# Cross-attention block on one core: a quarter of the W1 product by seven block products, and another order of the sum behind the W2 product

## The chip, the cores and the metric

The kernel runs on one core of a Trainium2 chip. The metric is device time in microseconds (us) of one execution. Five engines work side by side, each through its own list of instructions in the order written: TensorE (PE in the profile, with PEld for its weight loads), VectorE (DVE), ScalarE (ACT), GpSimd (POOL) and SyncE (SP), which here issues nearly all DMAs. They wait for each other by semaphores.

## What is computed

128 sequences of 128 tokens with 256 features pass one cross-attention block with 16 heads, two layer norms and a two-layer network with 1024 hidden features:

```python
q = (query @ Wq + bq).reshape(b, s, 16, 16).transpose(0, 2, 1, 3)     # k, v likewise, from the context
scores = jnp.einsum('bhqd,bhkd->bhqk', q, k) / 4
scores = jnp.where(j < i, scores, -1e30)                              # strictly below the diagonal
attn = softmax(scores).at[:, :, 0, :].set(0.0)
x = layer_norm(query + (attn @ v) @ Wo + bo, ln1_g, ln1_b)
ffn = jax.nn.relu(x @ W1 + b1) @ W2 + b2
out = layer_norm(x + ffn, ln2_g, ln2_b)
```

The part that the change touches is the line with `ffn`. All is float32.

## The kernel before

Two sequences make a pair, p = 0 to 63. From p = 7 on the function `step(p)` (line 1212) is one turn of a software pipeline: it does the scores and the softmax of pair p, projects the keys and queries of p + 1, weighs the values of p - 2 and sends them through Wo and the first norm, does the hidden layer of p - 3, the W2 product of p - 4 and the last norm of p - 5. The order is written out by hand: the framework keeps each engine's instructions in the order in which the calls stand. Steps 0 to 6 (`third` to `sixth`) fill the pipeline, `behind` (line 1278) empties it.

On PE one step is: `weigh` (L483, L493), `scores_both` (L376), `queries` (L261), `attention_out` (L512), `keys` (L261), `values` (L301), `second_by_seven` (L794), `hidden` (L699).

The W2 product is already done by seven block products: with the 1024 hidden features cut into even and odd blocks of 128, and the 256 tokens and the 256 outputs into halves, a product of 2 x 2 blocks needs seven block products instead of eight (Winograd's form of Strassen's scheme). Its sums of operands are `combine_hidden` (L780 to L783, on POOL) and once `combine_w2`; `second_by_seven` runs the seven products, each over four pairs of feature blocks, 128 columns wide, into two banks, `py` and `pz`. In each product, one empty instruction (`empty`, L215) follows the first call. `sum_of_seven` (line 813) adds the seven results and the residual `x1b` on DVE: four additions at L823 that each take one 128-wide part of `py` into 512, 384 or 256 elements of `t2`, and one at L831 for three parts of `pz`. Each of them has one operand in PSUM.

`hidden` (line 688) does the W1 product: eight feature blocks of 128, each as two calls of 256 columns (one for each half of the 256 inputs), two blocks to a bank; banks 2, 3, 4, 0 in turn; ACT then adds the bias and applies relu into `hT` (L707). A call in float32 shows as two records in the trace.

On DVE a step is: masks and maxima of the scores (L390, L743, L747, L754), sum and statistics of the first norm (L538, L525, L526), the softmax's sums and reciprocals (L421, L422), the block transposes `turn_x1` (L663) and `tokens` (L247), one `turn` (L436), `sum_of_seven`, two more `turn`, the statistics of the second norm (L525, L526). On POOL: deviation of the second norm (L532, L533, L577), `combine_hidden`, `add_bo` (L254), deviation of the first norm (again L532, L533, L577), three multiplies of the softmax by its reciprocal sums (`sums`, L423), `residual1` (L566, L569), `finish` (L597, L598). On ACT: the copy of the weighed values (L505), 32 exponentials (L762), queries (L272), first norm (L554), keys (L291), `values_out` (two copies L311, two L316), second norm (`norm2`, L591), eight relus (L707). On SP: `bring` (16 moves of the transposed softmax, L451), `store` (L606), loads, and the moves of `turn_x1` (L239, L242).

In step 7 alone, `norm2`, `finish` and `store` of pair 1 stand at the head of the step as well. The eight PSUM banks are used by fixed number; the scores of the second half of the queries take banks 0 to 3, those of the first half banks 6, 7, 4, 5, and a step's scores begin with banks 4 and 5. Queries go to bank 4, keys to 0, values to 1, `po` to 5, the weighed values to 7.

Of the kernel before, what the change touches and what calls it, by code (L numbers as in the profile page):

```python
# [19 lines left out]
def tile_cross_attention_block(  # L20
# [22 lines left out]
    nc = tc.nc  # L43
    B, S, D = x.shape
# [4 lines left out]
    KC = D // P  # L49
    FC = DFF // P  # L50
    TP = 2 * P
    NS = P // 32
# [10 lines left out]
    const = ctx.enter_context(tc.tile_pool(name="const", bufs=1))  # L63
    loads = ctx.enter_context(tc.tile_pool(name="loads", bufs=3))
# [60 lines left out]
    load_tokens(0, slice(0, 2))  # L125
    wk = weight(Wk, "wk")
    wq = weight(Wq, "wq")
    c_first = const.tile([P, 4, D], F32, tag="c_first", name="c_first")
# [81 lines left out]
    def at_bank(i, name):  # L210
        return psum.tile([P, 512], F32, tag=f"b{i}", name=name)
# [39 lines left out]
    def add_bo(p):  # L251
        st = states[p]
        st["xb"] = proj.tile([P, 2, D], F32, tag="xb", name=f"xb_{p}")
        nc.gpsimd.tensor_tensor(  # L254
            st["xb"], tokens_of[p // 2][:, p % 2 * 2 : p % 2 * 2 + 2], bov_r[:, None, :].to_broadcast([P, 2, D]), ALU.add
        )
# [47 lines left out]
                )  # L304

    def values_out(p):
        st = states[p]
        pv = st.pop("pv")
        st["vz"], st["vd"] = vzs[p % 2], vds[p % 2]
        for s in range(2):  # L310
            nc.scalar.copy(  # L311
                st["vz"][:, s, :, 0:4:3, :],
                pv[:, s * D : (s + 1) * D].rearrange("p (r e d) -> p r e d", e=2, d=DK),
            )
        for e in range(2):
# [69 lines left out]
    def mask(p, hi, rs):  # L385
        st = states[p]
        n = P if hi else HP
        no = neg.rearrange("p u j -> p (u j)") if hi else neg[:, 1, :]
        for r in rs:
            nc.vector.tensor_tensor(  # L390
                st["sm", hi][:, 4 * r : 4 * r + 4, :],
                st["sps", hi][r][:, : 4 * n].rearrange("p (n j) -> p n j", j=n),
                no[:, None, :].to_broadcast([P, 4, n]),
                ALU.add,
            )
# [389 lines left out]
    def second_by_seven(p):  # L785

        st = states[p]
        hT, hs = st["hT"], st["hS"]
        py = st["py"] = at_bank(6, f"py_{p}")
        pz = st["pz"] = at_bank(7, f"pz_{p}")  # L790

        def product(out, left, right, after):
            for k in range(FC // 2):
                nc.tensor.matmul(  # L794
                    out, left(k), right(k), start=(k == 0), stop=(k == FC // 2 - 1)
                )
# [10 lines left out]
        product(pz[:, 2 * P : 3 * P], raw(1, 1), lambda k: wt[:, 3, k], 1)  # L807
        product(py[:, 3 * P :], lambda k: hs[:, 0, k], lambda k: wt[:, 0, k], 1)
        product(py[:, 2 * P : 3 * P], lambda k: hs[:, 2, k], lambda k: wt[:, 2, k], 1)
        product(py[:, P : 2 * P], lambda k: hs[:, 1, k], lambda k: wt[:, 1, k], 1)  # L810
        product(pz[:, P : 2 * P], lambda k: hs[:, 3, k], weights(1, 1), 1)

    def sum_of_seven(p):

        st = states[p]
        t2 = st["t2"] = ffn.tile([P, 2, D], F32, tag="t2", name=f"t2_{p}")
        t = t2.rearrange("p s (h d) -> p (s h) d", h=2)
        py, pz = st.pop("py"), st.pop("pz")
        x1b = st.pop("x1b").rearrange("p s (h d) -> p (s h) d", h=2)

        def add(to, of, at):
            n = to.shape[1]
            nc.vector.tensor_tensor(  # L823
                to, of, py[:, None, at * P : (at + 1) * P].to_broadcast([P, n, P]), ALU.add
            )
# [5 lines left out]
        nc.vector.tensor_tensor(  # L831
            t[:, :3], t[:, :3], pz[:, : 3 * P].rearrange("p (n d) -> p n d", d=P), ALU.add
        )

    def second_half(p, s):

# [331 lines left out]
    def sixth(p):  # L1168

        weigh(p - 2)  # L1170
        context(p - 2)
        scores_both(p)
        add_bo(p - 1)
        mask(p, 0, B)
# [36 lines left out]

    def step(p):
        last = p == NP - 1
        weigh(p - 2)
        context(p - 2)
        scores_both(p)
        if p == 7:
            norm2(p - 6)
        combine_hidden(p - 4, POOL_ALONE)
        if p == 7:  # L1220
            finish(p - 6)
            store(p - 6)
# [148 lines left out]
```

## Time and profile before

| | us |
|---|---|
| median of three runs | 1527.93 (1526.05 to 1528.2) |
| the profiled execution | 1528.67 |
| its span, first to last instruction | 1527.0 |
| PE busy | 1514.3 |
| DVE busy | 1332.4 |
| POOL busy | 1255.9 |
| ACT busy | 1118.3 |

A line of the timeline has the start, the length from the first start to the last end, the engine, the line of the kernel, the operation, what it writes and reads, the shape and the count; in brackets, the idle time before it and what ended it. A line of the groups has, behind the bar, the busy time of the group in us and the mean ns of one instruction. A line of the chain of waits has start, share of the chain in us and the piece. "Idle" on an engine that is not the bound costs nothing.

### The profile page before, as it was taken

To read this page: it belongs to the slowest core of one execution; us is meant where nothing else is said; L and a number is where in the kernel's file an instruction comes from. 1 tells how busy PE (TensorE), PEld (TensorE's weight loads), DVE (VectorE), ACT (ScalarE), POOL (GpSimd) and SP (SyncE) were. 2 spreads that over 40 slices of the span, in tenths; PEclk is the share of its full clock that TensorE was granted. 3 is DMA by queue.
4 is the path that set the end of the run, shared out by engine and by line. 5 is a ranking of instruction groups with operands and counts; after the bars stand their busy time and mean duration, and the time that the engine had idled before them with its cause. 6 is when DMAs were issued, how large, how long until landed. Compare 5 with 4: busy or idle time off the path is not lost.

```text
span 1527.0 us, 47892 instructions
## 1 busy us (share of the span) xinstructions
PE 1514.3 (99%) x17926; PEld 1360.6 (89%) x17926; DVE 1332.4 (87%) x2498; ACT 1118.3 (73%) x3391; POOL 1255.9 (82%) x1282
## 2 busy tenths in 40 slices
PE   8999999999999999999999999999999999999998
PEld 7788998998989989989989899899899898998997
DVE  7989988988988988889889889889898898898885
ACT  5668777877877877778778778777777787787752
POOL 6876988888888888888888888888888888888883
PEclk9999999999999999999999999999999999999999
DMA  9356665555656656655556666566566566564441
GB/s 192 87 120 141 154 156 132 135 136 132 143 139 138 143 120 141 148 132 135 137 134 142 145 134 136 132 136 148 134 136 138 128 141 147 133 144 109 115 112 49
DMA packets 415285, 204.24 MB, mean 134 GB/s; under 512 B 282448, under 2 KB 383056, under 8 KB 415056
## 3 DMA queue, kind: packets, MB, share of 16 engines
q1 hardware_dynamic: 412768, 199.34, 56.7%
q8 instruction: 144, 2.36, 0.7%
q10 hardware_dynamic: 2288, 1.85, 0.5%
q14 instruction: 85, 0.70, 0.2%
HBM read 70.26 MB, written 33.29 MB: 68 GB/s over the span
## 4 chain that ended last, share of the span: by engine, by line
PE 94%; DVE 3%; POOL 1%; DMA 1%; issue 1%; ACT 0%; SPq 0%; POOLq 0%; DVEq 0%
PE ph L699 28%; PE py L794 14%; PE pz L794 10%; PE pq L261 7%; PE po L512 7%; PE pv L301 7%; PE pk L261 7%; PE pss L376 6%; PE pc L493 4%; PE pc L483 2%; DVE tb L436 1%; PE py L719 0%; DMA x1t<-tbx 0%; DVE sm L390 0%; DVE su L421 0%
## 5 line engine op out<-in xcount | busy, mean ns | idle before, releaser
L699 PE MATMUL ph<-x1T,w 128*128 128x256 f32 x2048 | 453.6, 380 | 0.7 <-DMA x1T<-x1t 0.7
L699 PEld LDWEIGHTS ph<-x1T,w 128*128 128x128 f32 x2048 | 385.0, 190 | 50.9 <-issue 1.2
L423 POOL TENSOR_TENSOR sm<-sm,rs 128x1024 f32<-128x1024 f32 x192 | 359.3, 1898 | 3.9 <-DVE rs L422 3.3
L762 ACT ACTIVATE sm<-pss,nmx 128x128 f32<-128x128 f32 x944 | 249.9, 414 | 127.3 <-DMA pT<-tb 81.0
L707 ACT ACTIVATE hT<-ph,b1e_c 128x256 f32<-128x256 f32 x504 | 209.1, 467 | 171.3 <-PE ph L699 161.3
L762 ACT ACTIVATE sm<-sm,nmx 128x64 f32<-128x64 f32 x944 | 232.2, 337 | 5.1 <-DVE nmx L754 0.3
L421 DVE TENSOR_REDUCE su<-sm 128x8 f32<-128x1024 f32 (+1 forms) x192 | 225.8, 1176 | 4.0 <-ACT sm L409 3.8
L436 DVE STREAM_TRANSPOSE tb<-sm 128x1024 f32<-128x1024 f32 x186 | 221.0, 1214 | 0.0
L390 DVE TENSOR_TENSOR sm<-pss,neg 128x256 f32<-128x256 f32 (+1 forms) x276 | 108.2, 435 | 121.2 <-PE pss L376 115.4
L532 POOL TENSOR_SCALAR ve<-mv 128x2 f32<-128x2 f32 x127 | 28.7, 226 | 191.7 <-DVE mv L526 190.9
L794 PE MATMUL py<-wt,hS 128*128 128x128 f32 x1440 | 170.6, 275 | 0.0
L794 PEld LDWEIGHTS py<-wt,hS 128*128 128x128 f32 x1440 | 165.7, 192 | 0.0
L747 DVE TENSOR_REDUCE nmx<-pss 128x4 f32<-128x512 f32 x236 | 150.8, 680 | 0.0
L261 PE MATMUL pq<-xT,wq 128*128 128x256 f32 x504 | 125.5, 392 | 0.5 <-DVE sm L390 0.5
L291 ACT ACTIVATE kT<-pk,bkh,half 128x256 f32<-128x256 f32 x252 | 120.3, 558 | 4.0 <-PE pk L261 4.0
L512 PE MATMUL po<-wo,cxT 128*128 128x256 f32 x512 | 121.3, 380 | 0.7 <-ACT cxT L505 0.7
L301 PE MATMUL pv<-wv,cT 128*128 128x256 f32 x512 | 121.0, 380 | 0.0
L261 PE MATMUL pk<-cT,wk 128*128 128x256 f32 x504 | 119.2, 380 | 0.0
L512 PEld LDWEIGHTS po<-wo,cxT 128*128 128x128 f32 x512 | 97.1, 190 | 14.3 <-ACT cxT L505 1.2
L261 PEld LDWEIGHTS pq<-xT,wq 128*128 128x128 f32 x504 | 90.9, 190 | 20.8 <-issue 9.6
L301 PEld LDWEIGHTS pv<-wv,cT 128*128 128x128 f32 x512 | 97.4, 190 | 13.0
L261 PEld LDWEIGHTS pk<-cT,wk 128*128 128x128 f32 x504 | 95.9, 190 | 13.0 <-issue 0.2
(135 smaller groups left out, 2966.6 us busy)
## 6 DMA issues: line engine op xcount, KB each, us to landing
pT<-tb SPq DMA_DIRECT2D x976, 96.0 KB
x1t<-tbx SPq DMA_DIRECT2D x252, 64.0 KB
x1T<-x1t SPq DMA_DIRECT2D x63, 256.0 KB
out_dram<-t SPq DMA_DIRECT2D x63, 256.0 KB
xb<-in_x_dram SPq DMA_DIRECT2D x124, 128.0 KB
cb<-in_ctx_dram SPq DMA_DIRECT2D x124, 128.0 KB
x<-in_x_dram SPq DMA_DIRECT2D x31, 512.0 KB
w<-in_L_xattn_W_dram SPq DMA_DIRECT2D x2, 1024.0 KB
```

Of the source, the lines that this page charges most:

```text
L261: nc.tensor.matmul(ps[:, m * TP : (m + 1) * TP], w[:, k, m * P : (m + 1) * P], src[:, k, :], start=(k == 0), stop=(k == KC - 1),)
L291: nc.scalar.activation(st["kT"][:, m, e, :], pk[:, m * TP : (m + 1) * TP], AF.Identity, bias=bkh[:, m, e : e + 1], scale=half[:, e : e + 1],)
L301: nc.tensor.matmul(pv[:, s * D : (s + 1) * D], st["cT"][:, k, s * P : (s + 1) * P], wv[:, k, :], start=(k == 0), stop=(k == KC - 1),)
L421: nc.vector.tensor_reduce(su, sm[:, part, :], AX.X, ALU.add)
L423: nc.gpsimd.tensor_tensor(sm[:, part, :], sm[:, part, :], rs[:, :, None].to_broadcast([P, part.stop - part.start, n]), ALU.mult,)
L436: nc.vector.transpose(st["tb"][:, :, at : at + 256].rearrange("p j (n a) -> p n j a", a=32), st["sm", hi].rearrange("p h j -> p (h j)")[:, ...
L512: nc.tensor.matmul(po[:, s * D : (s + 1) * D], cxT[:, k, s, :], wo[:, k, :], start=(k == 0), stop=(k == KC - 1),)
L699: nc.tensor.matmul(ph[:, i * TP : (i + 1) * TP].rearrange("p (s i a) -> p s i a", s=2, a=32), w1[:, k, (f + i) * P : (f + i + 1) * P], st[ ...
L707: nc.scalar.activation(st["hT"][:, f + i, :], ph[:, i * TP : (i + 1) * TP], AF.Relu, bias=(b1e_c if p else b1_c)[:, f + i : f + i + 1], sc ...
L747: nc.vector.tensor_reduce(st["nmx", 1][:, 4 * r : 4 * r + 4], st["sps", 1][r].rearrange("p (n j) -> p n j", j=P), AX.X, ALU.max, negate=True,)
L762: nc.scalar.activation(sm[:, h, :], src, AF.Exp, bias=nmx[:, h : h + 1], scale=1.0)
L794: nc.tensor.matmul(out, left(k), right(k), start=(k == 0), stop=(k == FC // 2 - 1))
```

## The change

Hidden feature blocks 0 and 1 are no longer computed by eight calls of 256 columns, but by seven block products of 128 columns in the scheme above: the two feature blocks, the two sequences of the pair (`s`) and the two halves of the input are the 2 x 2 blocks. Blocks 2 to 7 stay as they were (`plain`). This needs

- `combine_w1`, once, in the sixth step: four subtractions of weights on POOL;
- `combine_normed` in each step: four additions and subtractions of 128 elements on POOL, behind `add_bo`;
- seven calls of 128 columns on PE (`Hidden.run`);
- on ACT, a copy of the first product into `hT` (`keep`);
- on DVE, five additions (`u2`, `u3`, `rest`) that build the four blocks in `hT`, each with one product in PSUM; the relu of blocks 0 and 1 then reads and writes `hT`.

The sum behind the W2 product is another one: ACT copies the first product into a small tile `u` (`keep_first`), and DVE makes six additions, four of them on 128 or 256 elements; the third and the fourth add `x1b` and `u`, both in SBUF.

`values_out` is cut in two, with ACT's copies of `u` and of the first product between; `norm2` stands behind the additions of the hidden layer; the plain blocks go to banks 4, 0 and 5. The empty instructions of the W2 product are 9, 9, 9, 8, 8, 8, 8 instead of one in each. The first context tile `c_first` uses a buffer of the load pool instead of its own. `behind` keeps the old `hidden` and `sum_of_seven`.

```diff
     def values_out(p):
-        st = states[p]
-        pv = st.pop("pv")
+        spread_values(p)
+        stack_values(p)
...
-        product(py[:, :P], raw(0, 0), weights(0, 0), 1)
-        product(pz[:, :P], raw(1, 0), weights(1, 0), 1)
...
+        product(py[:, :P], raw(0, 0), weights(0, 0), 9)
+        product(pz[:, :P], raw(1, 0), weights(1, 0), 9)
...
+    def combine_normed(p):
+
+        st = states[p]
+        x1T = st["x1T"]
+        xs = st["xS"] = ffn.tile([P, 4, NS, 32], F32, tag="xS", name=f"xS_{p}", bufs=1)
+        nc.gpsimd.tensor_tensor(xs[:, 0], x1T[:, 1, :, 0, :], x1T[:, 1, :, 1, :], ALU.add)
+        nc.gpsimd.tensor_tensor(xs[:, 2], x1T[:, 0, :, 0, :], x1T[:, 1, :, 0, :], ALU.subtract)
+        nc.gpsimd.tensor_tensor(xs[:, 1], xs[:, 0], x1T[:, 0, :, 0, :], ALU.subtract)
+        nc.gpsimd.tensor_tensor(xs[:, 3], x1T[:, 0, :, 1, :], xs[:, 1], ALU.subtract)
...
+        def run(self, which):
...
+            ps = self.of(which)
+            for i in range(NI):
+                nc.tensor.matmul(
+                    ps[:, i * P : (i + 1) * P].rearrange("p (n a) -> p n a", a=32),
+                    left(i), right, start=True, stop=True,
+                )
...
+        def keep(self):
+            nc.scalar.copy(self.h[:, 0, 0], self.one(1))
+
+        def u2(self):
+            nc.vector.tensor_tensor(self.h[:, 1, 0], self.h[:, 0, 0], self.one(6), ALU.add)
+
+        def u3(self):
+            nc.vector.tensor_tensor(self.h[:, 1, 1], self.h[:, 1, 0], self.one(7), ALU.add)
+            nc.vector.tensor_tensor(self.h[:, 0, 1], self.h[:, 1, 1], self.one(4), ALU.add)
+
+        def rest(self):
+            odd = self.hT[:, 1 : 2 * NI : 2].rearrange("p i (s t) -> p i s t", s=2)
+            nc.vector.tensor_tensor(
+                odd, odd, self.one(5)[:, :, None, :].to_broadcast([P, NI, 2, P]), ALU.add
+            )
+            low = self.h[:, :, 0]
+            nc.vector.tensor_tensor(
+                low, low, self.of(2, 2).rearrange("p (e i t) -> p e i t", e=2, i=NI), ALU.add
+            )
...
+    def keep_first(p):
+        u = states[p]["u"] = ffn.tile([P, 3, P], F32, tag="u", name=f"u_{p}", bufs=1)
+        nc.scalar.copy(u[:, 0], states[p]["py"][:, :P])
+
+    def sum_of_products(p):
...
+        add(u[:, 1], u[:, 0], py[:, P : 2 * P])
+        add(u[:, 2], u[:, 1], py[:, 2 * P : 3 * P])
+        add(t[:, :3], x1b[:, :3], u)
+        add(t[:, 3], x1b[:, 3], u[:, 2])
+        add(t[:, 1::2], t[:, 1::2], py[:, None, 3 * P :].to_broadcast([P, 2, P]))
+        add(t[:, :3], t[:, :3], pz[:, : 3 * P].rearrange("p (n d) -> p n d", d=P))
...
         add_bo(p - 1)
+        combine_normed(p - 3)
         load_ahead(p)
...
         values(p)
-        values_out(p)
-        norm2(p - 5)
         sums(p, 1, ONE)
         sums(p, 1, TWO)
         sums(p, 0, ALL)
         turn_x1(p - 2)
         residual1(p - 3)
         second_by_seven(p - 4)
-        hidden(p - 3, range(FC))
+        spread_values(p)
+        keep_first(p - 4)
+        h = Hidden(p - 3)
+        h.run(1)
+        h.run(6)
+        h.run(7)
+        h.run(4)
+        h.keep()
+        stack_values(p)
...
         turn(p, 1, 0)
-        sum_of_seven(p - 4)
+        sum_of_products(p - 4)
+        h.u2()
+        h.u3()
+        h.run(2)
+        h.run(3)
+        h.run(5)
+        h.rest()
+        norm2(p - 5)
+        h.plain([2, 3], 4)
+        h.relu(2)
+        h.relu(3)
+        h.plain([4, 5], 0)
+        h.relu(4)
+        h.relu(5)
         turn(p, 1, 1)
+        for f in range(2 * NI):
+            h.relu(f)
+        h.plain([6, 7], 5)
+        h.relu(6)
+        h.relu(7)
         turn(p, 0, 0)
```

More of the change, by code (lines that the diff above doesn't have):

```diff
@@ L127, in tile_cross_attention_block @@
     wq = weight(Wq, "wq")
-    c_first = const.tile([P, 4, D], F32, tag="c_first", name="c_first")
+    c_first = loads.tile([P, 4, D], F32, tag="cb2", name="c_first", bufs=2)
     nc.scalar.dma_start(c_first[:, 0:2], c[0:2].rearrange("b p d -> p b d"))
@@ L306, in values_out, with spread_values @@
     def values_out(p):
+        spread_values(p)
+        stack_values(p)
+    def spread_values(p):
         st = states[p]
-        pv = st.pop("pv")
+        pv = st["pv"]
         st["vz"], st["vd"] = vzs[p % 2], vds[p % 2]
@@ L314, in values_out, with stack_values @@
             )
+    def stack_values(p):
+        st = states[p]
+        pv = st.pop("pv")
         for e in range(2):
@@ L803, in weights @@
             return lambda k: w2[:, 2 * k + e, h * P : (h + 1) * P]
-        product(py[:, :P], raw(0, 0), weights(0, 0), 1)
-        product(pz[:, :P], raw(1, 0), weights(1, 0), 1)
[L807 to L811, printed above, removed]
+        product(py[:, :P], raw(0, 0), weights(0, 0), 9)
+        product(pz[:, :P], raw(1, 0), weights(1, 0), 9)
+        product(pz[:, 2 * P : 3 * P], raw(1, 1), lambda k: wt[:, 3, k], 9)
+        product(py[:, 3 * P :], lambda k: hs[:, 0, k], lambda k: wt[:, 0, k], 8)
+        product(py[:, 2 * P : 3 * P], lambda k: hs[:, 2, k], lambda k: wt[:, 2, k], 8)
+        product(py[:, P : 2 * P], lambda k: hs[:, 1, k], lambda k: wt[:, 1, k], 8)
+        product(pz[:, P : 2 * P], lambda k: hs[:, 3, k], weights(1, 1), 8)
     def sum_of_seven(p):
@@ L833, in sum_of_seven, with combine_w1 @@
         )
+    NI = 1
+    w1t = const.tile([P, 4, NI, P], F32, tag="w1t", name="w1t")
+    def combine_w1():
+        w = w1.rearrange("p k (i e f) -> p k e i f", e=2, f=P)[:, :, :, :NI]
+        nc.gpsimd.tensor_tensor(w1t[:, 0], w[:, 0, 1], w[:, 0, 0], ALU.subtract)
+        nc.gpsimd.tensor_tensor(w1t[:, 1], w[:, 1, 1], w1t[:, 0], ALU.subtract)
+        nc.gpsimd.tensor_tensor(w1t[:, 2], w[:, 1, 1], w[:, 0, 1], ALU.subtract)
+        nc.gpsimd.tensor_tensor(w1t[:, 3], w[:, 1, 0], w1t[:, 1], ALU.subtract)
@@ new lines, in tile_cross_attention_block, with __init__, of, one @@
+    class Hidden:
+        WHERE = {1: (2, 0), 6: (2, 1), 7: (2, 2), 4: (2, 3), 2: (3, 0), 3: (3, 1), 5: (3, 2)}
+        def __init__(self, p):
+            st = states[p]
+            self.p, self.x1T, self.xs = p, st["x1T"], st["xS"]
+            self.hT = st["hT"] = ffn.tile([P, FC, TP], F32, tag="hT", name=f"hT_{p}", bufs=1)
+            self.h = self.hT[:, : 2 * NI].rearrange("p (i e) (s t) -> p e s i t", e=2, s=2)
+            self.banks, self.plains = {}, {}
+        def of(self, which, n=1):
+            at, n0 = self.WHERE[which]
+            if at not in self.banks:
+                self.banks[at] = at_bank(at, f"phs_{self.p}_{at}")
+            return self.banks[at][:, n0 * NI * P : (n0 + n) * NI * P]
+        def run(self, which):
+            raw = lambda s, k: self.x1T[:, s, :, k, :]
+            given = lambda k, e: lambda i: w1[:, k, (2 * i + e) * P : (2 * i + e + 1) * P]
+            xs, ws = lambda i: self.xs[:, i], lambda n: (lambda i: w1t[:, n, i])
+            right, left = {
+                1: (raw(0, 0), given(0, 0)), 2: (raw(0, 1), given(1, 0)),
+                3: (xs(3), given(1, 1)), 4: (raw(1, 1), ws(3)),
+                5: (xs(0), ws(0)), 6: (xs(1), ws(1)), 7: (xs(2), ws(2)),
+            }[which]
+            ps = self.of(which)
[4 more added lines that the diff above has]
+                )
+        def one(self, which):
+            return self.of(which).rearrange("p (i t) -> p i t", i=NI)
+        def keep(self):
[14 more added lines that the diff above has]
+            )
+        def relu(self, f):
+            nc.scalar.activation(
+                self.hT[:, f], self.plains.get(f, self.hT[:, f]), AF.Relu,
+                bias=b1e_c[:, f : f + 1], scale=1.0,
+            )
+        def plain(self, fs, at):
+            ps = at_bank(at, f"ph_{self.p}_{fs[0]}")
+            for i, f in enumerate(fs):
+                self.plains[f] = ps[:, i * TP : (i + 1) * TP]
+                for k in range(KC):
+                    nc.tensor.matmul(
+                        self.plains[f].rearrange("p (s i a) -> p s i a", s=2, a=32),
+                        w1[:, k, f * P : (f + 1) * P], self.x1T[:, :, :, k, :],
+                        start=(k == 0), stop=(k == KC - 1),
+                    )
@@ new lines, in keep_first, with add @@
+    def keep_first(p):
+        u = states[p]["u"] = ffn.tile([P, 3, P], F32, tag="u", name=f"u_{p}", bufs=1)
+        nc.scalar.copy(u[:, 0], states[p]["py"][:, :P])
+    def sum_of_products(p):
+        st = states[p]
+        t2 = st["t2"] = ffn.tile([P, 2, D], F32, tag="t2", name=f"t2_{p}")
+        t = t2.rearrange("p s (h d) -> p (s h) d", h=2)
+        py, pz, u = st.pop("py"), st.pop("pz"), st.pop("u")
+        x1b = st.pop("x1b").rearrange("p s (h d) -> p (s h) d", h=2)
+        def add(to, one, two):
+            nc.vector.tensor_tensor(to, one, two, ALU.add)
+        add(u[:, 1], u[:, 0], py[:, P : 2 * P])
[4 more added lines that the diff above has]
+        add(t[:, :3], t[:, :3], pz[:, : 3 * P].rearrange("p (n d) -> p n d", d=P))
@@ L1173, in sixth @@
         add_bo(p - 1)
+        combine_w1()
         mask(p, 0, B)
```

1 line of the change is left out of this document (added).

## The prediction

> **What bounds the kernel now.** I read the page's first and fourth parts, then the timeline of each engine over one step in the middle, then the groups.
>
> ```profile
> PE 1514.3 (99%) x17926; PEld 1360.6 (89%) x17926; DVE 1332.4 (87%) x2498; ACT 1118.3 (73%) x3391; POOL 1255.9 (82%) x1282
> PE 94%; DVE 3%; POOL 1%; DMA 1%; issue 1%; ACT 0%; SPq 0%; POOLq 0%; DVEq 0%
> ```
>
> TensorE (PE) is busy 99% and is 94% of the chain that ended last. Its timeline over one step:
>
> ```profile
> 726.03 0.43 PE L483 MATMUL pc<-pT,vd 128*32 128x64 f32 x16
> ...
> 729.06 2.00 PE L261 MATMUL pq<-xT,wq 128*128 128x256 f32 x8
> ...
> 742.32 7.07 PE L699 MATMUL ph<-x1T,w 128*128 128x256 f32 x32
> 749.32 0.43 PE L483 MATMUL pc<-pT,vd 128*32 128x64 f32 x16
> ```
>
> A step is 749.32 - 726.03 = 23.29 us, with no idle on PE; the queries start 3.03 into it. The chain of waits prices its pieces:
>
> ```profile
> 741.59 0.89 PE pz L794 x8
> 742.48 6.91 PE ph L699 x32
> ```
>
> One record with 128 columns is 0.89/8 = 0.1115 us, one with 256 columns 6.91/32 = 0.216 us. Next, VectorE (DVE) in the same step, and GpSimd (POOL):
>
> ```profile
> 726.02 0.18 DVE L526 BATCH_NORM_AGGREGATE mv<-bs 128x2 f32<-128x6 f32 x1
> 728.31 0.76 DVE L390 TENSOR_TENSOR sm<-pss,neg 128x256 f32<-128x256 f32 x2 [2.11 <-PE pss L376]
> ...
> 740.46 0.65 DVE L663 STREAM_TRANSPOSE tbx<-x 128x512 f32<-128x512 f32 x1
> ...
> 743.35 0.65 DVE L823 TENSOR_TENSOR t<-x1b,py 128x512 f32<-128x512 f32 x1
> 744.03 1.47 DVE L823 TENSOR_TENSOR t<-t,py 128x384 f32<-128x384 f32 x3
> 745.60 0.55 DVE L831 TENSOR_TENSOR t<-t,pz 128x384 f32<-128x384 f32 x1
> 746.07 2.37 DVE L436 STREAM_TRANSPOSE tb<-sm 128x1024 f32<-128x1024 f32 x2
> ...
> 749.31 0.18 DVE L526 BATCH_NORM_AGGREGATE mv<-bs 128x2 f32<-128x6 f32 x1
> ```
>
> ```profile
> 732.90 1.27 POOL L254 TENSOR_TENSOR xb<-x,bov_r 128x512 f32<-128x512 f32 x1
> 736.60 0.23 POOL L532 TENSOR_SCALAR ve<-mv 128x2 f32<-128x2 f32 x1 [2.43 <-DVE mv L526]
> ...
> 738.17 5.61 POOL L423 TENSOR_TENSOR sm<-sm,rs 128x1024 f32<-128x1024 f32 x3
> 743.74 1.27 POOL L566 TENSOR_TENSOR x1b<-x,g_r 128x512 f32<-128x512 f32 x1
> ```
>
> DVE works without a break from 728.31 to 749.49 (21.18 us) and idles 2.11. A late DVE cannot use all of that, as its first mask in a step waits on many semaphores; in step 8, where it is late, 0.19 passes (DVE's timeline there, then PE's):
>
> ```profile
> 163.25 0.69 DVE L823 TENSOR_TENSOR t<-x1b,py 128x512 f32<-128x512 f32 x1 [1.26 <-DMA out_dram<-t]
> ...
> 169.24 0.18 DVE L526 BATCH_NORM_AGGREGATE mv<-bs 128x2 f32<-128x6 f32 x1
> 169.61 0.76 DVE L390 TENSOR_TENSOR sm<-pss,neg 128x256 f32<-128x256 f32 x2 [0.19 <-DMA x1t<-tbx]
> ```
>
> ```profile
> 170.09 2.00 PE L261 MATMUL pq<-xT,wq 128*128 128x256 f32 x8 [0.23 <-DVE sm L390]
> ```
>
> So DVE alone could turn a step in 21.18 + 0.19 = 21.37 us. PE is the bound by 1.92 us a step: that is all that the change may add to DVE.
>
> **The change, part by part.** *PE's products.* Two feature blocks cost 8 records of 256 columns, 1.728 us; seven block products cost 14 records of 128, 1.561. PE saves 0.167 a step, over 57 steps 9.5 us; its step would be 23.12.
>
> *Empty instructions.* 59 a step instead of 7. The fourth stage has 44 of them inside one W1 product:
>
> ```profile
> 79.51 7.14 PE L699 MATMUL ph<-x1T,w 128*128 128x256 f32 x32 [0.67 <-DMA x1T<-x1t]
> ```
>
> ```profile
> L215 PEldq NOP  x44: 13/13/13, 79.5 to 83.7; - x44
> ```
>
> With them 32 records took 7.14, against 7.07 in the steady step without (742.32 above). The sequencer took at most 4.2/43 = 0.098 us per empty one, its share of the products included; nine beside a product of 0.89 us are 0.88, eight 0.78. They hide behind the array's own pace, and I cost them at nothing; uncovered they would be 52 x 0.098 = 5.1 us a step.
>
> *ScalarE (ACT).* Two small copies more, the second normalisation later.
>
> ```profile
> 739.28 1.08 ACT L554 ACTIVATE x<-t,nb,sd 128x256 f32<-128x256 f32 x2
> ...
> 745.98 0.84 ACT L707 ACTIVATE hT<-ph,b1e_c 128x256 f32<-128x256 f32 x2 [0.81 <-PE ph L699]
> ```
>
> ACT waits for PE before such a pair (0.81 here), and that time hides the copies; without it they would cost two of some 0.3 us each.
>
> *POOL: four subtractions of 128 elements.* No such size is in the trace; the neighbours are
>
> ```profile
> L971 POOL TENSOR_TENSOR be1b_r<-be_r,b_r 128x256 f32<-128x256 f32 x1 | 0.7, 727 | 0.0
> L780 POOL TENSOR_TENSOR hS<-hT 128x512 f32<-128x512 f32 x57 | 72.6, 1274 | 0.0
> ```
>
> that is 2.13 ns an element, 0.45 us for 128, about 1.75 for the four with the overlap of independent ones. They fill the 2.43 us that POOL waits at 736.60. That cover shrinks as DVE moves (below). After DVE's last statistics (726.20, call it D) POOL needs 7.97 to the end of L254 (734.17), 1.75 for the new four, 1.57 (736.60 to 738.17) to its three multiplies. These then stand from D + 11.29 to D + 16.90, at 1.87 each, the third from D + 15.03. The first normalisation waits for POOL too (1.4 of the 1.57), takes 1.08, and frees DVE's transpose L663 at about D + 12.2; DVE itself comes there at D + 0.19 + 12.15. Even, so nothing is added, but another 0.2 us on POOL would be.
>
> The queue of SyncE starts its block moves later by what DVE is later (1.7 us and more); weigh reads them two steps on, so 20 us cover it. The first context tile in a load buffer, and the new weight combinations in the sixth stage, fall where POOL idles 9 us (waits: longest of L532, 9.0):
>
> ```profile
> POOL ve L532 <- DVE mv L526: 190.9, 118, 9.0
> ```
>
> *DVE: eleven additions instead of five.* Prices by elements with a PSUM operand:
>
> ```profile
> L823 DVE TENSOR_TENSOR t<-t,py 128x256 f32<-128x256 f32 x120 | 50.5, 421 | 4.1
> L823 DVE TENSOR_TENSOR t<-t,py 128x384 f32<-128x384 f32 x60 | 33.3, 555 | 2.1
> ```
>
> 1.05 ns an element, so 0.29 us for 128. A dependent next one starts 0.035 after the end, 0.10 if it also waits for another engine (745.50 to 745.60 above), an independent one 0.08 before it (746.15 to 746.07). The new sum: 0.32 + 0.39 + 0.47 + 0.32 + 0.53 + 0.47 = 2.50. The hidden layer's five: 3 x 0.39 (each waits for a product of its own) + 0.46 + 0.34 = 1.97. Together 4.47 where the old sum took 746.07 - 743.35 = 2.72: **1.75 us more**, with bounds of 1.55 (no extra gaps) and 1.95. DVE's own loop becomes 21.37 + 1.75 = 23.12, level with PE's 23.12. There is nothing left for a wait.
>
> *The wait that I expect.* The third and fourth additions of the new sum (x1b and u) read both operands from SBUF. In the steady steps of before, no DVE addition does: each has a PSUM operand. (In the groups: L390 and L743 add to pss, L538 to po, L823 to py, L831 to pz.) Only in the tail does DVE combine hidden values with two SBUF operands while POOL works. DVE, then POOL, then PE:
>
> ```profile
> 1470.87 0.96 DVE L780 TENSOR_TENSOR hS<-hT 128x512 f32<-128x512 f32 x1
> 1471.76 0.68 DVE L781 TENSOR_TENSOR hS<-hT 128x512 f32<-128x512 f32 x1
> ```
>
> ```profile
> 1470.02 1.27 POOL L598 TENSOR_TENSOR t<-t,be_r 128x512 f32<-128x512 f32 x1
> 1471.38 0.54 POOL L532 TENSOR_SCALAR ve<-mv 128x2 f32<-128x2 f32 x1
> ```
>
> ```profile
> 1472.34 2.84 PE L794 MATMUL py<-wt,hS 128*128 128x128 f32 x24
> ```
>
> The first took 0.96 instead of 0.68: POOL's L598 had 0.42 to run when it started, and it lost 0.28 of these (0.14 is its own lead). POOL's L532, behind it, took 0.54 instead of 0.23. So the two exclude each other. In the changed step the third addition comes at D + 0.19 + 15.04 (728.31 to 743.35) + 0.71 = D + 15.94, inside POOL's third multiply, which ends at D + 16.90: 0.96 left, **0.81 us lost**. For the fourth, the ends are 0 (L781, right behind, ran at 0.68) and 1.13 (POOL's waiting L566 of 1.27 gets in between); I take 0, the row of a DVE operation, and keep the other.
>
> The Trainium skill, "SBUF — State Buffer", section "SBUF: two separate sides", says that a DVE operation with two SBUF inputs and a GpSimd operation that reads SBUF lock the same port pair, for the whole instruction and whoever starts first. By that rule alone the whole 0.96 would be lost, some 8 us more over the run; the trace agrees but for the lead of 0.14.
>
> *Sum.* Step: 23.12 + 0.81 = 23.93, 0.64 over 23.29. 53 periods (steps 9 to 61): +33.9. Steps 7 and 8: in step 7 finish and add_bo hold POOL, so the new four delay L532 by 1.6; DVE's 1.26 idle at 163.25 takes most of it (0.25 left). DVE ends 0.25 + 1.75 + 0.81 = 2.8 later, at 172.2; its mask releases the queries at 172.9 instead of 170.1 (they want 169.6): +2.9, less 0.3 of PE's saving, +2.6. The last two steps have less DVE work: -0.3. Behind step 63 DVE combines hidden values for PE (done at 1471.83, wanted by PE at 1472.34, above), and comes up to 2.5 later, with 0.5 to spare: +2.0. Altogether +38.2. The profiled execution took 1528.67 (span 1527.0), 0.7 over the median 1527.93; 1528.67 + 38.2 = **1567**.
>
> **The rivals.**
> 1. *Not slower: the third addition meets no busy port* (POOL's multiplies past, or the exclusion smaller for a short operation). It decides from a wait of 0.1 us a step. Then PE's 23.12 holds: -9.5, +2.2 at steps 7 and 8, +1.3 in the tail: 1522.7. For: the exclusion of a DVE operation rests on one row. Against: POOL works without a break from D + 9.7 to the end of the step.
> 2. *POOL gets in between the two additions*: 1.13 more, step 25.06, 54 x 1.13 = 61 more: 1628. For: POOL's L532 ended 0.08 after the first DVE operation, before the second was done. Against: L781 lost nothing by it.
> 3. *A short wait, 0.05 to 0.15*: DVE takes back what PE saves; 1526 to 1531, no difference.
> 4. *The empty instructions are not hidden*: one that held the array for its 0.013 us costs 52 x 0.013 = 0.7 a step, less PE's saving 0.5, 1558 even if DVE lost nothing; at the sequencer's 0.098, 5.1 a step, 1810. The row with 44 of them speaks against both.
>
> **How the numbers follow.** Forecast (one wait, 0.4 to 1.0 us) 0.42; rival 1 0.26; rival 2 0.20; rival 3 0.07; rival 4 and the rest 0.05. About 0.2%, 3 us, is what a measurement of this kernel can tell from no change. Faster 0.26, within 0.07, slower 0.42 + 0.20 + 0.05 = 0.67. The forecast's own range is 1545 to 1578 (waits of 0.4 to 1.0, the additions 1.55 to 1.95 where they matter). To hold 8 in 10 it must reach to rival 1, 1518, and take in rival 2 up to 1640.
>
> **What would show it.** Right: steps of 23.9 with PE idle some 0.8 in each, released by DVE; the third addition (out of x1b and u) lasting 1.3 instead of 0.55, with POOL's L423 beside it; no idle on DVE but 0.2. Wrong: steps of 23.12 with DVE idle ahead of L390; or the addition at 0.55 while POOL works, which kills the reason; the fourth at over 1 us would be rival 2; records of the array spread beside the empty instructions rival 4.

## The result, and the profile after

The changed kernel takes **1628.91 us** (median of 4 runs, 1628.61 to 1633.73); the kernel before took 1528.07 beside it. The ratio is 1.067, interval 1.065 to 1.069: slower by 101 us, where the forecast had 38. It is the time of the second rival, 1628. The profiled execution took 1633.73, its span 1632.0.

The page's first part, then PE's timeline over one step (start, length, engine, line; in brackets the idle time ahead and what ended it). Line numbers are those of the changed kernel: weigh is L491, scores L384, the seven W2 products L802, the seven W1 products L892, the plain W1 product L931.

```profile
PE 1535.9 (94%) x18268; PEld 1373.7 (84%) x18268; DVE 1527.9 (94%) x2840; ACT 1148.8 (70%) x3505; POOL 1373.9 (84%) x1514
```

```profile
747.11 0.43 PE L491 MATMUL pc<-pT,vd 128*32 128x64 f32 x16
...
749.78 1.61 PE L384 MATMUL pss<-kT,qT 32*64 32x128 f32 x62 [0.77 <-ACT hT L921]
752.01 1.99 PE L261 MATMUL pq<-xT,wq 128*128 128x256 f32 x8 [0.61 <-DVE sm L398]
...
772.11 0.43 PE L491 MATMUL pc<-pT,vd 128*32 128x64 f32 x16
```

A step takes 772.11 - 747.11 = 25.00 us instead of 23.29, and PE, 99% busy before, is at 94% and waits twice in it: ahead of the scores for ACT's relu, which itself waits for DVE's additions of the hidden layer, and ahead of the queries for DVE's mask. Both come from DVE. Its timeline (the last statistics of the step before, then the second half of this one), then POOL's beside it:

```profile
751.16 0.18 DVE L534 BATCH_NORM_AGGREGATE mv<-bs 128x2 f32<-128x6 f32 x1
...
763.73 0.71 DVE L671 STREAM_TRANSPOSE tbx<-x 128x512 f32<-128x512 f32 x1
...
765.55 1.20 DVE L444 STREAM_TRANSPOSE tb<-sm 128x1024 f32<-128x1024 f32 x1
766.67 0.57 DVE L950 TENSOR_TENSOR u<-u,py 128x128 f32<-128x128 f32 x2
767.28 2.78 DVE L950 TENSOR_TENSOR t<-x1b,u 128x384 f32<-128x384 f32 x2
770.10 0.42 DVE L950 TENSOR_TENSOR t<-t,py 128x256 f32<-128x256 f32 x1
770.62 0.56 DVE L950 TENSOR_TENSOR t<-t,pz 128x384 f32<-128x384 f32 x1
771.09 0.28 DVE L904 TENSOR_TENSOR hT<-hT,phs 128x128 f32<-128x128 f32 x1
...
772.91 2.36 DVE L444 STREAM_TRANSPOSE tb<-sm 128x1024 f32<-128x1024 f32 x2
```

```profile
758.05 1.27 POOL L254 TENSOR_TENSOR xb<-x,bov_r 128x512 f32<-128x512 f32 x1
...
760.64 0.45 POOL L862 TENSOR_TENSOR xS<-x1T,xS 128x128 f32<-128x128 f32 x1
761.18 0.23 POOL L540 TENSOR_SCALAR ve<-mv 128x2 f32<-128x2 f32 x1
...
762.76 5.61 POOL L431 TENSOR_TENSOR sm<-sm,rs 128x1024 f32<-128x1024 f32 x3
768.33 1.58 POOL L574 TENSOR_TENSOR x1b<-x,g_r 128x512 f32<-128x512 f32 x1
769.99 1.27 POOL L577 TENSOR_TENSOR x1b<-x1b,be1b_r 128x512 f32<-128x512 f32 x1
```

The two additions of x1b and u take 2.78 us together where their sizes alone would want 0.8. The third starts at 767.28, while POOL's third multiplication runs to 768.37: 1.09 us are left of it. The addition ends at 768.78, after 1.50 instead of 0.55, so it loses 0.95 of the 1.09. POOL's next instruction, L574, began at 768.33 and takes 1.58 instead of 1.27, so that it ends at 769.91; the fourth addition ends at 770.06, 0.15 later. The groups give the means over the run, that of POOL's multiplication from both kernels (L431 here, L423 before; behind the bar: busy time, mean ns of one):

```profile
L950 DVE TENSOR_TENSOR t<-x1b,u 128x384 f32<-128x384 f32 x57 | 86.7, 1522 | 2.1
L950 DVE TENSOR_TENSOR t<-x1b,u 128x128 f32<-128x128 f32 x57 | 77.3, 1355 | 0.0
...
L431 POOL TENSOR_TENSOR sm<-sm,rs 128x1024 f32<-128x1024 f32 x192 | 359.6, 1900 | 3.6 <-DVE rs L430 3.3
...
L574 POOL TENSOR_TENSOR x1b<-x,g_r 128x512 f32<-128x512 f32 x63 | 98.2, 1559 | 0.0
```

```profile
L423 POOL TENSOR_TENSOR sm<-sm,rs 128x1024 f32<-128x1024 f32 x192 | 359.3, 1898 | 3.9 <-DVE rs L422 3.3
```

The multiplication that the third addition waits for isn't slowed itself: 1.900 us in the mean against 1.898 before.

### The profile page after: what moved, and what is told of

Read it like the earlier page. It is cut to its first block, busy times and chain, and to the rows that moved or that the text cites. A ratio compares the mean times of both kernels' runs of the same rounds, so it can differ in the third digit from the quotient of the medians.

```text
span 1632.0 us, 52503 instructions
## 1 busy us (share of the span) xinstructions
PE 1535.9 (94%) x18268; PEld 1373.7 (84%) x18268; DVE 1527.9 (94%) x2840; ACT 1148.8 (70%) x3505; POOL 1373.9 (84%) x1514
## 3 DMA queue, kind: packets, MB, share of 16 engines
q8 instruction: 159, 2.61, 0.7%
## 5 line engine op out<-in xcount | busy, mean ns | idle before, releaser
L431 POOL TENSOR_TENSOR sm<-sm,rs 128x1024 f32<-128x1024 f32 x192 | 359.6, 1900 | 3.6 <-DVE rs L430 3.3
L931 PE MATMUL ph<-x1T,w 128*128 128x256 f32 x1368 | 304.8, 379 | 1.7 <-ACT vd L324 1.7
L931 PEld LDWEIGHTS ph<-x1T,w 128*128 128x128 f32 x1368 | 255.6, 190 | 34.2 <-ACT vd L324 1.9
L921 ACT ACTIVATE hT<-ph,b1e_c 128x256 f32<-128x256 f32 x342 | 142.2, 466 | 69.0 <-PE ph L931 69.0
L802 PE MATMUL py<-wt,hS 128*128 128x128 f32 x1440 | 170.6, 275 | 0.0
L802 PEld LDWEIGHTS py<-wt,hS 128*128 128x128 f32 x1440 | 165.6, 192 | 0.0
L384 PE MATMUL pss<-kT,qT 32*64 32x256 f32 (+1 forms) x3840 | 121.7, 330 | 44.3 <-ACT hT L921 43.7
L950 DVE TENSOR_TENSOR t<-x1b,u 128x384 f32<-128x384 f32 x114 | 159.6, 1439 | 2.1
L384 PEld LDWEIGHTS pss<-kT,qT 32*64 32x64 f32 x3840 | 90.9, 131 | 66.4 <-ACT hT L921 57.2
L921 ACT ACTIVATE hT<-hT,b1e_c 128x256 f32<-128x256 f32 x114 | 51.8, 501 | 103.9 <-DVE hT L916 103.9
```

The costliest lines, as they stand in the source:

```text
L384: nc.tensor.matmul(st["sps", hi][r][s * HP : (s + 1) * HP, m * 2 * n : (m + 1) * 2 * n].rearrange("p (e j) -> p e j", e=2), st["qT"][strip ...
L431: nc.gpsimd.tensor_tensor(sm[:, part, :], sm[:, part, :], rs[:, :, None].to_broadcast([P, part.stop - part.start, n]), ALU.mult,)
L802: nc.tensor.matmul(out, left(k), right(k), start=(k == 0), stop=(k == FC // 2 - 1))
L921: nc.scalar.activation(self.hT[:, f], self.plains.get(f, self.hT[:, f]), AF.Relu, bias=b1e_c[:, f : f + 1], scale=1.0,)
L931: nc.tensor.matmul(self.plains[f].rearrange("p (s i a) -> p s i a", s=2, a=32), w1[:, k, f * P : (f + 1) * P], self.x1T[:, :, :, k, :], st ...
L950: nc.vector.tensor_tensor(to, one, two, ALU.add)
```

## The experiments

The first theory: a DVE addition with both operands in SBUF and a POOL instruction exclude each other, each for its whole length, and POOL's waiting instruction goes first when DVE's addition ends. Its rivals: the two share ports in proportion; the added work alone makes DVE late; the empty instructions cost time. The times:

| | us | ratio to before, interval |
|---|---|---|
| changed kernel | 1628.91 | 1.0669 [1.0647, 1.0692] |
| old sum, new hidden layer | 1532.42 | 1.0022 [1.0013, 1.0031] |
| sums kept in PSUM | 1522.41 | 0.9961 [0.9949, 0.9974] |
| the same, 7 empty instructions | 1528.57 | 1.0003 [0.9994, 1.0012] |
| new sum alone, late copy | 1590.35 | 1.0402 [1.0386, 1.0418] |
| new sum alone, early copy | 1536.04 | 1.0047 [1.0031, 1.0064] |
| POOL's multiplication in halves | 1598.57 | 1.0458 [1.0444, 1.0473] |
| one addition instead of two | 1564.45 | 1.0236 [1.0222, 1.0250] |
| PSUM, block boundary moved | 1551.7 | 1.0155 [1.0142, 1.0169] |
| PSUM, both ends mended | 1526.75 | 0.9994 [0.9985, 1.0003] |
| PSUM, old last step | 1521.13 | 0.9955 [0.9942, 0.9969] |

**The old sum beside the new hidden layer.**

```diff
-        keep_first(p - 4)
...
-        sum_of_products(p - 4)
+        sum_of_seven(p - 4)
```

> The changed kernel with the old sum behind the W2 product (five additions, each with an operand in PSUM); the hidden layer by seven products stays. Theory: no VectorE addition has two SBUF operands, so no exclusion; VectorE's loop is 21.37 + 1.82 (the five additions of the hidden layer as the trace of after has them, 771.09 to 772.92) = 23.19 us, just over TensorE's 23.12; 1523 to 1530 us. Rival A (too many additions on VectorE): ten instead of eleven, but larger ones, so as slow as the changed kernel or slower, 1620 to 1640. Rival C (empties): 1629.

Measured 1532.42, steps of 23.28: 96 of the 101 us go with the new sum. DVE is now the bound by itself: its first mask waits only its usual 0.19.

```profile
754.45 0.76 DVE L398 TENSOR_TENSOR sm<-pss,neg 128x256 f32<-128x256 f32 x2 [0.19 <-PE pss L384]
```

So the five additions of the hidden layer cost DVE 23.28 - 21.37 = 1.91 us a step, and use up the spare time that DVE had.

**The same eleven additions, with a PSUM operand in each.** ACT copies products 1 and 3 instead of product 1 alone; u1 and u2 are written back into `py`.

```diff
-        nc.scalar.copy(u[:, 0], states[p]["py"][:, :P])
+        nc.scalar.copy(u[:, 0::2], ...(py, parts 0 and 2))
...
-        add(u[:, 1], u[:, 0], py[:, P : 2 * P])
-        add(u[:, 2], u[:, 1], py[:, 2 * P : 3 * P])
-        add(t[:, :3], x1b[:, :3], u)
-        add(t[:, 3], x1b[:, 3], u[:, 2])
+        add(v[:, 1], u[:, 0], v[:, 1])      # v: py as parts of 128
+        add(v[:, 2], u[:, 2], v[:, 1])
+        add(t[:, :3], x1b[:, :3], v)
+        add(t[:, 3], x1b[:, 3], v[:, 2])
```

> The changed kernel with the partial sums u1 and u2 left in PSUM: ACT copies products 1 and 3 out of py, VectorE writes the two partial sums back into py, and the two additions of x1b then take their second operand from PSUM. The same eleven VectorE additions of the same sizes. Theory (a VectorE addition with both operands in SBUF and a GpSimd operation that reads SBUF exclude each other): the two additions fall from 1.50 and 1.36 us to about 0.55 and 0.29, a step from 25.0 to 23.12 to 23.2 us, with TensorE the bound again; 1520 to 1527 us. Rival A (VectorE simply has too many additions): the step stays near 25, 1615 to 1630. Rival B (the additions wait for x1b from GpSimd): they stay long, 1629. Rival C (the 59 empty instructions): no change, 1629.

Measured 1522.41, steps of 23.127: PE's own pace, within 0.01 of the 23.12 that the prediction has for the case without a wait. Its DVE timeline, then POOL's:

```profile
764.64 0.75 DVE L950 TENSOR_TENSOR t<-x1b,py 128x384 f32<-128x384 f32 x2
...
772.10 0.76 DVE L398 TENSOR_TENSOR sm<-pss,neg 128x256 f32<-128x256 f32 x2 [0.44 <-PE pss L384]
```

```profile
760.02 5.61 POOL L431 TENSOR_TENSOR sm<-sm,rs 128x1024 f32<-128x1024 f32 x3
```

The multiplications run to 765.63, past the end of both additions. The groups:

```profile
L950 DVE TENSOR_TENSOR t<-x1b,py 128x384 f32<-128x384 f32 x57 | 31.6, 554 | 2.0
L950 DVE TENSOR_TENSOR t<-x1b,py 128x128 f32<-128x128 f32 x57 | 15.9, 279 | 0.0
...
L574 POOL TENSOR_TENSOR x1b<-x,g_r 128x512 f32<-128x512 f32 x63 | 80.3, 1275 | 0.0
```

Same additions, same sizes, same POOL instructions beside them: 0.55 and 0.28 us instead of 1.52 and 1.36, and POOL's L574 is back at 1.275. **The third addition lost 0.97 us, the fourth 1.08, and POOL's multiplication 0.28**, and what decides is where the second operand lies. That the added work alone makes DVE late falls.

**POOL's multiplication in two halves.**

```diff
-        engine.tensor_tensor(x1b, st["x1"], g1_r..., ALU.mult)
+        for s in range(2):
+            engine.tensor_tensor(x1b[:, s], st["x1"][:, s], g1_r, ALU.mult)
```

> The changed kernel with POOL's multiplication by the first gain (512 elements, L574) written as two of 256. Theory (a POOL instruction that waits for the third addition gets the ports at its end and keeps them for the whole of itself): the fourth addition waits for 0.73 us (256 elements) instead of 1.27, so it loses 0.53 instead of 1.07; steps of 24.46 instead of 25.00, 54 x 0.54 = 29 us less, 1600. Rival (the two engines share the ports in proportion while both work): 1629 as before. If the second half also gets in ahead of the fourth addition: 1629 too, with both halves beside it in the timeline.

Measured 1598.57, steps of 24.45; in the groups of this version:

```profile
L949 DVE TENSOR_TENSOR t<-x1b,u 128x384 f32<-128x384 f32 x57 | 87.5, 1535 | 2.0
L949 DVE TENSOR_TENSOR t<-x1b,u 128x128 f32<-128x128 f32 x57 | 46.3, 813 | 0.0
```

The third addition is unchanged, the fourth loses 0.813 - 0.279 = 0.53 instead of 1.08. DVE's code is the same; only the length of the POOL instruction that stands between the two additions was halved. The second half does not get in as well: when the first ends, the waiting addition goes.

**One addition instead of two.** u2 is written twice (256 elements), so that x1b + u is one addition of 512.

```diff
-        add(u[:, 2], u[:, 1], py[:, 2 * P : 3 * P])
-        add(t[:, :3], x1b[:, :3], u)
-        add(t[:, 3], x1b[:, 3], u[:, 2])
+        add(u[:, 2:], ...(u1 twice), ...(third part of py twice))
+        add(t, x1b, u)
```

> The changed kernel with u2 written twice (256 elements, +0.13 us) so that x1b + u is one addition of 512 instead of two (0.69 instead of 0.87). Theory (only the gap between the third and the fourth addition let POOL in): 0.95 us lost to the third multiplication stays, the 1.07 of the fourth goes, 0.05 less work: steps of 23.9 and 1568 us, the time that was forecast. Rival (the additions are slowed in proportion to their elements): steps of 25.0, 1629.

Measured 1564.45, steps of 23.85. Groups, then DVE's timeline and POOL's:

```profile
L950 DVE TENSOR_TENSOR t<-x1b,u 128x512 f32<-128x512 f32 x57 | 86.9, 1524 | 1.9
```

```profile
761.45 1.50 DVE L950 TENSOR_TENSOR t<-x1b,u 128x512 f32<-128x512 f32 x1
```

```profile
756.79 5.62 POOL L431 TENSOR_TENSOR sm<-sm,rs 128x1024 f32<-128x1024 f32 x3
762.36 1.72 POOL L574 TENSOR_TENSOR x1b<-x,g_r 128x512 f32<-128x512 f32 x1
```

The addition starts at 761.45, when POOL's multiplication, which runs to 762.41, has 0.96 left. By its elements it would take 0.69; it takes 1.50, so it loses 0.81 (the mean over the run is 1.524). The smaller addition of the changed kernel lost more, 0.95, because 1.09 were left when it started: the loss is what POOL's instruction has left, less 0.14, and not a share of the addition's own elements. That 1.524 is so near the 1.522 of the changed kernel is chance. The shared-port rival falls, also because the multiplication itself keeps its 1.900. And the forecast had just this: 0.96 left and 0.81 lost; its step, 23.93, and its time, 1567, lie close to those of this version, which has one wait and not two.

**The new sum alone, twice.** The kernel before with `sum_of_products` and its copy; first with the copy behind the second normalisation on ACT, then (same sum) with the W2 product and the copy called ahead of `values_out`:

```diff
+        second_by_seven(p - 4)
+        keep_first(p - 4)
         values_out(p)
         norm2(p - 5)
...
-        second_by_seven(p - 4)
-        keep_first(p - 4)
         hidden(p - 3, range(FC))
```

> The kernel before with the new sum behind the W2 product alone (ACT's copy and the six additions, two of them with both operands in SBUF); hidden layer, empties and all else as before. Theory: the two additions are long here too (1.3 to 1.5 us each), VectorE has 2.0 - 0.2 = 1.8 us more to do in a step, and its spare of 1.92 just covers it: steps of 23.29, 1526 to 1532 us, VectorE's idle ahead of its first mask down to 0.2 to 0.4. Rival B (the additions wait for x1b): they are short here, since x1b has the same head start; idle 2.2. A time over 1540 would mean that the loss is larger than the spare.

Measured 1590.35, far over what was expected; the placement of the copy did it. DVE's timeline:

```profile
748.40 0.61 DVE L848 TENSOR_TENSOR u<-u,py 128x128 f32<-128x128 f32 x2 [1.20 <-ACT u L837]
749.04 2.78 DVE L848 TENSOR_TENSOR t<-x1b,u 128x384 f32<-128x384 f32 x2
```

DVE waited 1.20 us in each step for ACT's copy, which stood behind the normalisation. With the copy early:

> The kernel before with the new sum alone, its copy of the first product now ahead of the copies of the values on ACT, so that VectorE does not wait for it. Theory: VectorE's loop is 24.37 - 1.20 = 23.17, under PE's 23.29: steps of 23.29, 1526 to 1530. The additions come 1.20 earlier; if they then meet the second and the third multiplication, they lose up to 0.3 more, 23.5 and 1540. Rival (the new sum costs its step in any placement): 24.37, 1590.

Measured 1536.04, with 43 of the 54 steps in the middle at 23.290, PE's pace; the profiled execution took 1532.88. The additions lose the same 2.0 us, to other POOL instructions: DVE's timeline, then POOL's.

```profile
722.14 2.75 DVE L848 TENSOR_TENSOR t<-x1b,u 128x384 f32<-128x384 f32 x2
...
729.78 0.76 DVE L390 TENSOR_TENSOR sm<-pss,neg 128x256 f32<-128x256 f32 x2 [0.45 <-PE pss L376]
```

```profile
721.92 1.27 POOL L566 TENSOR_TENSOR x1b<-x,g_r 128x512 f32<-128x512 f32 x1
723.27 1.46 POOL L569 TENSOR_TENSOR x1b<-x1b,be1b_r 128x512 f32<-128x512 f32 x1
```

Now the third addition comes 0.22 behind the start of L566 and waits for it, and L569 (1.46 instead of the 1.27 of the kernel before) goes between the two. But DVE still idles 0.45 ahead of its mask: without the hidden layer's additions the loss fits into its spare time. So neither half of the change costs much alone; together they cost 101 us, since the first takes the spare time away that hides the second. The 5 to 8 us above 1528 are single steps of 23.4 to 23.9 and a last step of 20.8 (19.9 before); what makes the unprofiled runs 3 us longer than the profiled one is open.

**The empty instructions.** The version in PSUM with one empty instruction a product, as in the kernel before (7 instead of 59 a step):

```diff
-        product(py[:, :P], raw(0, 0), weights(0, 0), 9)
+        product(py[:, :P], raw(0, 0), weights(0, 0), 1)
...
```

> The run with the partial sums in PSUM, and seven empty instructions a step as in the kernel before instead of 59. Theory (the empties hide behind the array's pace): within 0.2% of the run with 59, 1520 to 1527 us. Rival (each empty holds the array for 0.013 us or more): 52 fewer make it 0.7 us a step faster wherever TensorE is the bound, some 38 us less than the run with 59. Third possibility (the empties keep the step's instruction count a multiple of 64, and that count matters): single steps with a pause of TensorE of some tenths of a us, 2 to 15 us more than with 59.

Measured 1528.57: 6 us more. The steps stay at 23.128, but five of them are 0.75 to 1.0 longer, and so is the last one by 1.2. Its waits of PE (us in all, times, longest), and PE's timeline at one of them:

```profile
PE pss L384 <- issue: 2.8, 5, 0.9
```

```profile
587.16 1.57 PE L384 MATMUL pss<-kT,qT 32*64 32x128 f32 x56
589.34 0.45 PE L384 MATMUL pss<-kT,qT 32*64 32x128 f32 x8 [0.61 <-issue]
```

PE stops within the scores, and nothing that the profile shows holds it. I counted the instructions of TensorE in the trace (weight loads, products, empty ones, semaphores): 640 a step with 59 empty ones, 588 with 7. In the five long steps the pauses come at instructions 301, 305, 313, 317 and 321, in the last step at 309, and each of these is a multiple of 256 from the others in the whole program. (The one at 321 stands ahead of the queries, and the list of waits has it under DVE.) The page's third part shows such blocks: packets and MB of the queue that brings instructions.

```profile
q8 instruction: 159, 2.61, 0.7%
```

That is the changed kernel's: 2.61 MB in 159 packets, 16.4 KB each, and 159 x 256 = 40,704, where the trace has 40,697 instructions on TensorE. The version with 7 has 37,577 instructions and 147 packets. With 588 a step the block boundary wanders through the step; with 640 it alternates between two sets of places (85, 341, 597 and 213, 469), none of them at 301 to 321. The test moves the boundaries and leaves the steps as they are: empty instructions beside the W1 products of the sixth stage, once.

```diff
                     if p == 1:
                         empty(3 if f else 2)
+                    if p == 3:
+                        empty(2)
```

> The version with the sum in PSUM (59 empty instructions, 640 a step, 1522.4), with 64 more empty instructions beside the W1 products of the sixth stage, hidden there, nothing else. In the version with 7 empty ones the pauses stood where a multiple of 256 TensorE instructions (counted from the program's start) fell at the end of the scores, instruction 297 to 321 of a step; with 640 a step it falls at 85, 213, 341, 469, 597 in turn. Theory A (a block of 256 is late): 64 more move these to 21, 149, 277, 405, 533: none at 297 to 321, so 1522 to 1523, unless 277 pauses too: then every fourth to second step is 0.7 to 1.0 longer, 1532 to 1548. Theory B (only that 640 is a multiple of 128 or 64 counts): 1522.

The stage has 16 such calls, so 32 instructions came in, not 64, and the boundaries moved by 32: to 309 and 53, in every second step. Measured 1551.7. PE's waits and its timeline there:

```profile
PE pss L384 <- issue: 20.2, 27, 1.5
```

```profile
736.26 1.57 PE L384 MATMUL pss<-kT,qT 32*64 32x128 f32 x58
738.49 0.44 PE L384 MATMUL pss<-kT,qT 32*64 32x128 f32 x6 [0.67 <-issue]
738.86 1.99 PE L261 MATMUL pq<-xT,wq 128*128 128x256 f32 x8
```

27 pauses, in every second step of the 54 and in no other; the number of instructions in a step is the same 640. They last 0.4 to 1.5 us as idle time of PE, and in each of them TensorE goes on 1.2 to 1.7 us after a packet of the instruction queue has landed, which fits a block that comes late; no run moved the packets alone. So the empty ones cost nothing, as the prediction had it, and buy something that it did not see: a fixed place for the boundary. Theory B, that only the multiple counts, falls. Of theory A the place of the boundary is shown to decide; its times were for a boundary at 277, which this run did not make.

**The ends.** The PSUM version still has two long stretches, steps 7 and 8 and the last step.

```diff
-        if p == 7:
-            finish(p - 6)
-            store(p - 6)
         add_bo(p - 1)
-        combine_normed(p - 3)
+        if not last:
+            combine_normed(p - 3)
...
         shift(p - 2, 1)
+        if p == 7:
+            finish(p - 6)
+            store(p - 6)
...
+        if last:
+            ...(values_out, hidden, sum_of_seven as before)
```

> The version with the sum in PSUM (1522.4), with the two stretches mended that are still longer than in the kernel before: in step 7 POOL's finish of pair 1 comes behind the deviation and shift that the first normalisation waits for (the step after took 25.53, and VectorE idled 2.52 there ahead of L671), and the last step takes the old hidden layer and the old sum (it took 21.33 where the kernel before took 19.90). Theory: 0.9 to 2.3 us less at step 8, about 1.3 less in the last step: 1519 to 1520.5. Rival (another wait, POOL's multiplications above all, is as late): 1522.

Measured 1526.75, no gain: the last step fell to 19.90, but steps 7 and 8 rose from 23.5 and 25.5 to 28.4 and 26.8. DVE's timeline there:

```profile
169.95 0.75 DVE L950 TENSOR_TENSOR t<-x1b,py 128x384 f32<-128x384 f32 x2 [6.09 <-DMA out_dram<-t]
```

The later finish stores pair 1 later, and the new sum writes into the buffer that this store reads. With the last step alone:

> The version with the sum in PSUM (1522.4) with step 7 as it was there, and the old hidden layer and the old sum in the last step alone. The version with both ends mended had a last step of 19.90 instead of 21.33, and lost 6 us at step 7, where the later finish held the buffer that the new sum writes (VectorE idled 6.09 on the store). Theory: 1522.4 - 1.4 = 1521.0, ratio 0.995. Rival (the last step's gain is given back behind it): 1522.4.

Measured 1521.13, last step 19.90; the fastest version, 0.45% under the kernel before (interval 0.31 to 0.58%).

## Why the prediction was wrong

Its sign was right, and 1628.91 is in the wide range that was to hold 8 in 10 (1518 to 1640), but far outside the forecast's own (1545 to 1578): rival 2 happened, which had 0.20.

- *PE's saving.* Right: 23.12 foretold, 23.127 measured in the PSUM version.
- *The empty instructions at nothing.* Right for their cost. That leaving them out costs 6 us was not in it.
- *POOL's four subtractions.* 0.45 us each, as worked out, but together 1.86 (from the end of L254 at 759.32 to 761.18) instead of 1.75. POOL's wait ahead of the deviation is gone, and DVE's transposition L671 does not wait. Even, as it said.
- *DVE's added work.* 1.75 foretold, some 1.6 measured: 25.00 - 0.97 - 1.08 = 22.95, less 21.37. The five additions of the hidden layer took from 771.09 to the next instruction at 772.91, 1.82 instead of 1.97.
- *The third addition, "inside POOL's third multiply".* The place and the reason were right, and so was the lead of 0.14: with 1.09 left, 0.95 were lost in the step shown (0.97 in the mean). What was off by 0.13 is where POOL stood. D, the end of DVE's last statistics, is 751.34 here; the addition came at D + 15.94, as foretold, but the multiplication ended at D + 17.03 instead of D + 16.90, nearly all of it by the four subtractions. By the rule of the Trainium skill alone ("SBUF — State Buffer", "SBUF: two separate sides": whoever starts first has the port pair for the whole instruction) the whole 1.09 would have been lost. That the 0.96 which the prediction had by it is so near the 0.97 measured is luck.
- *The fourth addition, "I take 0".* **This is the step that failed.** It lost 1.08; the upper end, 1.13, was the answer. The row for 0 was L781, which ran at 0.68 right behind L780. But POOL's L532 had got in between these two: the prediction itself noted that it ended 0.08 behind the first. It works on 2 elements a partition and had only 0.16 left when L781 started (1471.76 to 1471.92), so that, less the lead of 0.14, L781 had next to nothing to lose. L566 (L574 in the changed kernel) works on 512 and takes 1.27. The halves (0.53 lost) and the single addition (nothing lost behind it) show the rule: at the end of a DVE addition the waiting POOL instruction goes next, though DVE's own next one is ready. 1.08 x 54 = 58 us of the 63 that the forecast lacked.
- *The rest.* Steps 7 and 8: +3.8 instead of +2.6. The last step and what follows: +4.2 and +1.6 instead of +1.7 together. The last step has the new sum and the new hidden layer too, and besides the usual two waits PE loses 1.67 there (L931 at 1565.45) to ACT's late copy of the values, which the sum did not have. Against these, the steps were 0.06 shorter than rival 2 had them (added work 0.17 less, the third addition's loss 0.16 more, the fourth's 0.05 less). So it is in part luck that its 1628 is so close; its mechanism is what happened.

The sum in its new form, from the rows: 21.37 + 1.6 + 0.97 + 1.08 = 25.0, less 23.29, by 54 steps = 92; 3.8 + 5.9 at the ends: 102 against 101 measured.

## What to carry to other kernels

Where VectorE works beside a busy GpSimd, keep one operand of every addition in PSUM, or make one long addition of several short ones with both in SBUF: each such instruction can wait for a whole GpSimd instruction, also behind another one of its own. Price an exclusion by the longest instruction that can stand in the gap, and not by a row in which a very short one stood there. And a loss in an engine's spare time costs nothing until another part of the change uses that time up: add the parts up for each engine before judging one.

## What the runs showed of the hardware

- DVE additions with both operands in SBUF and POOL's instructions of these runs exclude each other by whole instructions, and the turns alternate. An addition loses what the POOL instruction has left when it starts, less some 0.14 us: 0.95 of 1.09 (384 elements), 0.81 of 0.96 (512 elements). With an operand in PSUM the one of 384 took 0.554. POOL pays too (1.58 and 1.72 in the timelines instead of 1.27).
- TensorE's instructions arrive in blocks of 256. Where a boundary falls at instruction 301 to 321 of the step, at the end of weigh and scores (160 short products with their loads, 3.0 us in the PSUM version), the step gets 0.75 to 1.9 us longer; at 341, a few long products later, it doesn't. The Trainium skill, "Runtime: NRT & Kernel Launch", "Instruction fetch mechanics", says that an engine's sequencer fetches blocks of 256 instructions through its own queue, mostly hidden. The traces agree on the size; here it is hidden or not by the place of the boundary, worth 29 us between two versions that differ by 32 empty instructions outside the loop. Why the steps with a boundary at 297 and 325 stay at 23.13 us, and those from 301 to 321 don't, wasn't settled.
